# Attention in split float32: two narrow matmuls of the last key tile joined in a bank of their own, and half of the probabilities' low part made on GpSimd

## The chip, the core and the metric

The kernel runs on one core of one Trainium2 chip. Its time is the device time of one execution in microseconds (us). The engines are named as in the profile: PE is TensorE (matmuls), PEld its weight loads, DVE is VectorE, ACT is ScalarE, POOL is GpSimd, SP is SyncE, which here only starts DMAs. Each engine works through its own instructions in the order in which the program gives them; where one waits, those behind it on that engine wait too.

## The reference, cut to what matters

Four batches of 512 rows, 512 wide. The input is layer-normalised, and the normalised rows go through an attention of 16 heads and through a gated feed-forward network; the result is the input plus the product of both.

```python
x  = L0_attn_x                                   # (4, 512, 512)
xn = layernorm(x)
q = einsum('bpd,hde->bphe', xn, W_Q) + b_Q       # k and v alike; 16 heads of 128
scores = where(causal, einsum('bqhe,bkhe->bhqk', q, k) / sqrt(128), -100000.0)
attn = softmax(scores)
z = einsum('bkhe,bhqk->bqhe', v, attn)
s = einsum('bqhe,hed->bqd', z, W_O) + b_O
g = silu((silu((xn @ gate_w.T) * gate_s) * ((xn @ up_w.T) * up_s)) @ down_w.T * down_s)
out = x + s * g
```

## The kernel before, in words

**Split numbers.** Every operand of a matmul is kept as two float32r numbers, a high part (the value cast to float32r) and a low part (the value minus the high part, `Split` in line 28). A product of two such operands is three matmuls: high by high, low by high and high by low (`mm3`, line 90). The high part is usually written by ScalarE and the low part by VectorE, which needs the high part for its subtraction; weights have their low part from GpSimd (`split_w`, line 133).

**The order of the work.** The attention runs inside a manual schedule: the order in the program text is the order on each engine, and the tile framework adds the semaphores. The outer loop (line 525) goes over 64 heads, in the order group of two heads, batch, head of the group. In the iteration of head n stand, one after another:

- `softmax` (line 272): the scores of head n in four query tiles, packed in three PSUM tiles, only the causal part; VectorE adds the mask and takes the row minimum (L298); ScalarE takes the exponential (L312); VectorE the reciprocal of the row sum (L315); GpSimd multiplies by it (L316).
- `look` (a VectorE operation on feed-forward weights, from head 9 on) and the first half of `fill`: projections of v for an even head (`project_v`, L237 and L238 are its evacuations), or output projections of the group before for an odd one (`project_out`, L413).
- `turn_p` (line 319): VectorE transposes the probabilities in 32 by 32 blocks (L330), and a DMA to memory and four back by SyncE's queue finish the transposition. The result is used one head later.
- `split_p` (line 346) for head n-1: the probabilities that have come back, 128 by 4 by 320, are cast in two halves by ScalarE (L357) and their low parts made in two halves by VectorE (L358). In heads 1 to 3 and in the last one it stands before the fill (in head 1 before the softmax), from head 4 on behind `turn_p`.
- `split_pending`: weights that are due are split (ScalarE L134, GpSimd L135); then loads of later weights are started on ScalarE's queue (`prepare_qk`, `prepare_v`, `prepare_o`), which take the staging buffers that the splits before have freed.
- `project` for q and then k of head n+1 (L252 and L255 evacuate).
- `attend` (line 376) for head n-1: the product of v and the probabilities, the step that is changed.
- the second half of `fill`. In heads 0, 2 and 4 the normalised input of the next batch is also transposed (`ln_transpose`, `ln_low`, L222 to L225), and layer-norm statistics and normalisation (L187, L188, L194, L214) stand in heads 0 to 4.

The last head's probabilities are transposed on TensorE instead (`transpose_p`, line 366).

**The attention product before.** Probabilities lie transposed, key rows on the partitions, in ten blocks of 128 by 128: for key tile j the query tiles j to 3. So key tile 0 has a moving operand 512 wide, tile 1 384, tile 2 256 and tile 3, the last, 128. `attend` issues twelve matmuls into one PSUM bank z: for high by high, low by high and high by low the key tiles 0, 3, 1 and 2. Then ScalarE writes the high part of the 512 wide result with the bias (L391) and VectorE its low part (L392).

**Buffers.** PSUM has three banks of the pool `ps_st` (scores and half of the transposed inputs) and five of `ps_mm`, taken in turn by the projections, the output projections, z and the other transposed inputs. The probabilities' high and low parts are two tiles with one buffer each.

**The feed-forward part** follows, for all four batches, with its own order; its weights come by DMAs that GpSimd starts. It is not touched.

Of the kernel before, what the change touches and what calls it, by code (L numbers as in the profile page):

```python
# [10 lines left out]
F32 = mybir.dt.float32  # L11
F32R = mybir.dt.float32r
I32 = mybir.dt.int32
AF = mybir.ActivationFunctionType
ALU = mybir.AluOpType
# [3 lines left out]
P = 128  # L19
HG = 2  # L20
# [22 lines left out]
def kernel(  # L43
# [21 lines left out]
    nc = tc.nc  # L65
    B, S, D = x.shape
    H, E = w_o.shape[0], w_o.shape[1]
    NF = gate_w.shape[0]
    ND = D // P
    NT = S // P  # L70
# [25 lines left out]
    with ExitStack() as at:  # L96
        lnp = at.enter_context(tc.tile_pool(name="lnp", bufs=NT))
        small = at.enter_context(tc.tile_pool(name="small", bufs=8))
# [5 lines left out]
        pp = at.enter_context(tc.tile_pool(name="pp", bufs=1))  # L104
# [3 lines left out]
        ps_mm = at.enter_context(tc.tile_pool(name="ps_mm", bufs=5, space=PSUM))  # L108
# [31 lines left out]
        def weight(pool, shape, name, tag):  # L140
            return Split(
                pool.tile(shape, F32R, name=name + "h", tag=tag + "h"),
                pool.tile(shape, F32R, name=name + "l", tag=tag + "l"),
            )
# [123 lines left out]
        NS = NT * (NT + 1) // 2  # L268
        row = [t * (t + 1) // 2 * P for t in range(NT)]
        slot = [j * NT - j * (j - 1) // 2 for j in range(NT)]  # L270
# [48 lines left out]
        def turn_p(of):  # L319
# [23 lines left out]
                )  # L343
            return raw

        def split_p(raw):
            pt = weight(pp, [P, NS, P], "pt", "pt")
            half = NQ // 2
            for k in range(0, NQ, half):
                src = raw[:, k : k + half].rearrange("p b (s i) -> p b s i", i=Q)  # L350

                def dst(part):
                    return part[:, :, k * Q : (k + half) * Q].rearrange(
                        "p s (b i) -> p b s i", i=Q
                    )

                nc.scalar.copy(dst(pt.hi), src)  # L357
                nc.vector.tensor_tensor(dst(pt.lo), src, dst(pt.hi32), ALU.subtract)  # L358
            return pt

        def transpose_p(of):

            pt = weight(pp, [P, NS, P], "pt", "pt")
            pairs = [(j, t) for j in range(NT) for t in range(j, NT)]
            for s0 in range(0, NS, NT):
                n = min(NT, NS - s0)
                tr = ps_st.tile([P, n, P], F32, name="trp", tag="st")
                for k in range(n):
                    j, t = pairs[s0 + k]
                    nc.tensor.transpose(tr[:, k, :], of[t][:, ts(j, P)], ident)  # L370
                to = pt[:, s0 : s0 + n, :]
                nc.scalar.copy(to.hi, tr)
                nc.vector.tensor_tensor(to.lo, tr, to.hi32, ALU.subtract)
            return pt

        def attend(h, pt, vs):
            z = ps_mm.tile([P, NT, P], F32, name="z", tag="mm")


            todo = []  # L380
            for part, other in (("hi", "hi"), ("lo", "hi"), ("hi", "lo")):
                for j in (0, NT - 1, 1, 2):
                    v = getattr(vs[j], part)[:, ts(h % HG, E)]
                    p_ = getattr(pt, other)[:, slot[j] : slot[j] + NT - j, :]
                    todo.append((z[:, j:, :], v, p_))
            for k, (o, v, p_) in enumerate(todo):
                nc.tensor.matmul(o, v, p_, start=k == 0, stop=k == len(todo) - 1)  # L387
            zT = weight(zp, [P, NT, P], f"z{h}", "z")

            bias = bv_sb[:, h : h + 1]  # L390
            nc.scalar.activation(zT.hi, z, AF.Identity, bias=bias)  # L391
            nc.vector.scalar_tensor_tensor(zT.lo, z, bias, zT.hi32, ALU.add, ALU.subtract)  # L392
            return zT

        acc_in = {}
# [65 lines left out]
        with tc.manual_schedule():  # L461
# [59 lines left out]
            def attend_last(before, pt):  # L521
                g, b, i = before
                zs.setdefault((g, b), []).append(attend(g * HG + i, pt, v_of[g, b]))

            for n, (g, b, i) in enumerate(heads):
                h = g * HG + i
# [20 lines left out]
                if n == 1:  # L547
                    pt = split_p(raw)
                of = softmax(qT, kT)
                if n > 1 and early:  # L550
                    pt = split_p(raw)
# [5 lines left out]
                if not early:  # L557
                    pt = split_p(raw)
# [54 lines left out]
                if nxt is None:  # L613
                    pt = transpose_p(of)
# [6 lines left out]
                if n == len(heads) - 3:  # L621
                    inexact = any_of(low)
            last = (NG - 1, B - 1)
            zs[last].append(attend(H - 1, pt, v_of[last]))
            for t in range(NT):
                project_out(*last, t, zs[last])
# [177 lines left out]
```

## Time and profile before

| | us |
|---|---|
| median of 3 runs | 1223.65 (1223.3 to 1223.92) |
| the profiled execution | 1222.41 |
| its span | 1220.6 |
| PE busy | 1206.5 (99%) |
| DVE busy | 827.1 (68%) |
| ACT busy | 525.3 (43%) |
| POOL busy | 301.7 (25%) |
| granted TensorE clock, mean | 0.998 |

Groups of the profile that the change touches:

| line, engine | what | count | mean ns |
|---|---|---|---|
| L387 PE | attention product, 128 wide, high parts | 64 | 220 |
| L387 PE | the same, 256 / 384 / 512 wide | 64 each | 281 / 391 / 389 |
| L391 ACT | high part of z, 128x512 | 64 | 685 to 689 |
| L392 DVE | low part of z, 128x512 | 64 | 748 to 751 |
| L357 ACT | high part of the probabilities, 128x640 | 126 | 724 |
| L358 DVE | low part of the probabilities, 128x640 | 126 | 1099 (min 772, median 811, max 1916) |
| L135 POOL | low part of a weight, 128x512 | single rows | 1292 to 1879 |
| L316 POOL | normalisation, 128x512 / 128x128 | 64 each | 694 / 409 |

How to read it: a span is the time from the first to the last instruction of the profiled execution, and the execution's own time is a little longer. A matmul's duration includes its way through the array, in which the next one already runs; what it costs is the distance between starts. The mean of L358 hides two kinds of instance, as its median and maximum show. In a row of the timeline the columns are start in us from the span's start, duration in us, engine, line, operation, output and inputs, shape, and in brackets how long the engine had stood idle and what ended that.

### The profile page before, as it was taken

The numbers are of one execution on the slowest core, as the hardware profiler recorded it, in microseconds if no ns is written. First come the engines' busy times: TensorE is split into PE (matmuls) and PEld (weight loads), VectorE is DVE, ScalarE is ACT, GpSimd is POOL, SyncE is SP. The second block draws the span as 40 slices with busy tenths as digits, with TensorE's granted clock in tenths as the row PEclk, the third lists the DMA queues.
The fourth block names the chain that finished last, engine by engine and source line by source line (L and its number), as shares of the span: only waits on it lengthen the run. The fifth ranks groups of instructions, "written<-read, shape, count | busy, mean of one in ns | idle before, by whom it ended". The sixth has DMA issues, their size and how long they took to land.

```text
span 1220.6 us, 18887 instructions
## 1 busy us (share of the span) xinstructions
PE 1206.5 (99%) x6514; PEld 1052.7 (86%) x6514; DVE 827.1 (68%) x2044; ACT 525.3 (43%) x1169; POOL 301.7 (25%) x433
## 2 busy tenths in 40 slices
PE   8999999999999999999999999999999999999997
PEld 8888888888888888888888888888888888888886
DVE  6897777777777777777877676767677533434343
ACT  5654444444445445444544454445444342323231
POOL 4212321232123213321412141214121341212010
PEclk9999999999999999999999999999999999999999
DMA  4454456656665667566655565555544893627241
GB/s 161 138 175 147 145 165 206 206 179 190 190 207 174 203 198 218 181 208 192 211 182 173 178 189 175 177 185 173 173 156 156 272 317 93 207 87 213 80 147 38
DMA packets 117912, 215.55 MB, mean 177 GB/s; under 512 B 13232, under 2 KB 45744, under 8 KB 117808
## 3 DMA queue, kind: packets, MB, share of 16 engines
q1 hardware_dynamic: 74016, 134.51, 34.4%
q10 hardware_dynamic: 29376, 53.26, 14.2%
q0 software_dynamic: 14416, 26.48, 7.9%
q8 instruction: 53, 0.87, 0.3%
q14 instruction: 51, 0.42, 0.1%
HBM read 135.17 MB, written 79.04 MB: 175 GB/s over the span
## 4 chain that ended last, share of the span: by engine, by line
PE 95%; DVE 3%; ACT 1%; DMA 0%; issue 0%; SPq 0%; DVEq 0%; ACTq 0%
PE z L387 10%; PE pd L667 7%; PE pg L667 7%; PE pu L667 7%; PE pso L91 5%; PE psv L91 5%; PE pso L92 5%; PE pso L93 5%; PE psv L93 5%; PE psv L92 5%; PE psq L91 5%; PE psq L92 5%; PE psq L93 5%; PE psk L91 5%; PE psk L92 5%; PE psk L93 5%
## 5 line engine op out<-in xcount | busy, mean ns | idle before, releaser
L316 POOL TENSOR_SCALAR p<-p,rtot 128x512 f32<-128x512 f32 (+3 forms) x256 | 148.2, 598 | 675.1 <-DVE rtot L315 675.1
L312 ACT ACTIVATE p<-p,nmax 128x512 f32<-128x512 f32 (+3 forms) x256 | 140.9, 552 | 147.3 <-DVE nmax L298 147.3
L358 DVE TENSOR_TENSOR ptl<-ptr,pth 128x640 fp32r<-128x640 f32 x126 | 133.7, 1099 | 1.4 <-ACT pth L357 1.4
L330 DVE STREAM_TRANSPOSE sq<-p 128x256 f32<-128x256 f32 x378 | 113.3, 361 | 0.0
L298 DVE CUSTOM_DVE_ANT_0 p<-sc,mask 128x512 f32<-128x512 f32 (+2 forms) x192 | 96.5, 552 | 0.3 <-PE sc L93 0.3
L252 ACT ACTIVATE k<-psk,consts 128x512 fp32r<-128x512 f32 (+1 forms) x65 | 44.2, 681 | 108.7 <-PE psk L93 108.6
L252 ACT ACTIVATE q<-psq,consts 128x512 fp32r<-128x512 f32 (+1 forms) x65 | 44.3, 682 | 97.2 <-PE psq L93 72.6
L357 ACT CAST pth<-ptr 128x640 fp32r<-128x640 f32 x126 | 84.9, 724 | 0.1
L413 DVE TENSOR_TENSOR a<-pso,a 128x512 f32<-128x512 f32 x108 | 72.1, 686 | 17.7 <-PE pso L93 16.4
L255 DVE SCALAR_TENSOR_TENSOR k<-psk,consts,k 128x512 fp32r<-128x512 f32 (+1 forms) x65 | 48.0, 739 | 52.8 <-ACT k L252 52.7
L693 DVE SCALAR_TENSOR_TENSOR hd<-pu,consts,sg 128x512 f32<-128x512 f32 x44 | 33.0, 751 | 66.8 <-PE pu L667 62.2
L315 DVE RECIPROCAL rtot<-tot 128x1 f32<-128x1 f32 x256 | 41.6, 162 | 42.7 <-ACT p L312 36.3
L91 PE MATMUL sc<-k,q 128*128 128x512 f32 (+2 forms) x192 | 65.7, 342 | 1.7 <-DVE xl L225 1.7
L93 PE MATMUL sc<-k,q 128*128 128x512 f32 (+2 forms) x192 | 64.7, 337 | 0.0
L92 PE MATMUL sc<-k,q 128*128 128x512 f32 (+2 forms) x192 | 64.7, 337 | 0.0
L255 DVE SCALAR_TENSOR_TENSOR q<-psq,consts,q 128x512 fp32r<-128x512 f32 (+1 forms) x65 | 47.6, 732 | 7.6 <-ACT q L252 7.6
L312 ACT ACTIVATION_READ_ACCUMULATOR p<-p,nmax 128x1 f32 x256 | 47.8, 187 | 0.0
L91 PEld LDWEIGHTS sc<-k,q 128*128 128x128 f32 x192 | 36.2, 188 | 7.9 <-DVE xl L225 3.5
L723 ACT ACTIVATE o<-o 128x512 f32<-128x512 f32 (+1 forms) x17 | 10.3, 607 | 68.8 <-DVE o L722 68.8
L92 PEld LDWEIGHTS sc<-k,q 128*128 128x128 f32 x192 | 36.2, 189 | 3.6
L93 PEld LDWEIGHTS sc<-k,q 128*128 128x128 f32 x192 | 36.1, 188 | 2.6
L691 ACT ACTIVATE sg<-pg,consts 128x512 f32<-128x512 f32 x44 | 30.3, 688 | 17.0 <-PE pg L667 17.0
(734 smaller groups left out, 3811.6 us busy)
## 6 DMA issues: line engine op xcount, KB each, us to landing
turn<-sq SPq DMA_DIRECT2D x63, 640.0 KB, 3.8
ptr<-turn SPq DMA_DIRECT2D x252, 160.0 KB, 3.4
acc<-a SPq DMA_DIRECT2D x124, 256.0 KB, 3.7
a<-acc ACTq DMA_DIRECT2D x108, 256.0 KB, 2.8
xt<-in_x SPq DMA_DIRECT2D x16, 256.0 KB, 4.1
wor<-in_w_o ACTq DMA_DIRECT2D x16, 256.0 KB, 4.5
fa<-acc SPq DMA_DIRECT2D x16, 256.0 KB, 5.9
fx<-in_x SPq DMA_DIRECT2D x16, 256.0 KB, 6.9
```

What stands on the lines that cost most here:

```text
L91: nc.tensor.matmul(ps, a.hi, b.lo, start=first, stop=False)
L92: nc.tensor.matmul(ps, a.hi, b.hi, start=False, stop=False)
L93: nc.tensor.matmul(ps, a.lo, b.hi, start=False, stop=last)
L252: nc.scalar.activation(q.hi[:, at_], ps[:, at_], AF.Identity, bias=bias[:, h : h + 1])
L255: nc.vector.scalar_tensor_tensor(q.lo[:, at_], ps[:, at_], bias[:, h : h + 1], q.hi32[:, at_], ALU.add, ALU.subtract,)
L298: nc.vector.tensor_tensor_reduce(out=of[t], in0=where[t], in1=add, scale=-SCALE, scalar=BIG, op0=ALU.add, op1=ALU.min, accum_out=nmax[t],)
L312: nc.scalar.activation(of[t], of[t], AF.Exp, bias=nmax[t], scale=-1.0, accum_out=tot)
L316: nc.gpsimd.tensor_scalar(of[t], of[t], rtot, 1.0, ALU.mult, ALU.mult)
L330: nc.vector.transpose(dst.rearrange("p a s i -> p s a i"), src.rearrange("p (s a i) -> p s a i", s=n, i=Q),)
L358: nc.vector.tensor_tensor(dst(pt.lo), src, dst(pt.hi32), ALU.subtract)
L387: nc.tensor.matmul(o, v, p_, start=k == 0, stop=k == len(todo) - 1)
L667: nc.tensor.matmul(ps, l, r, start=first and k == 0, stop=last and k == len(pairs) - 1)
```

## The change

Three things change, all in the attention.

- `attend`: key tiles 0 to 2 go into z as before, in nine matmuls. The last key tile goes into a second bank, z2, 128 by 2 by 128. One matmul, 256 wide, multiplies the high part of v's last tile with the high and the low part of the probabilities' block, which lie side by side in the result; one, 128 wide, adds the low part of v times the high part of the probabilities to the first of the two. So eleven matmuls stand in place of twelve.
- The result leaves in two pieces: query tiles 0 to 2 from z as before, 384 wide; for the last query tile ScalarE copies z2 to memory on the chip (`rest`), VectorE adds its two halves and then the last part of z, and from that sum ScalarE writes the high and VectorE the low part, 128 wide.
- The probabilities' two parts are one tile with a high and a low half (`p_split`), since the joined matmul reads both; and of the two subtractions that make the low part (`split_p`) the first is GpSimd's and the second VectorE's.

```diff
+        def p_split():
+            both = pp.tile([P, 2, NS, P], F32R, name="pt", tag="pt")
+            pt = Split(both[:, 0], both[:, 1])
+            pt.both = both
+            return pt
+
         def split_p(raw):
-            pt = weight(pp, [P, NS, P], "pt", "pt")
+            pt = p_split()
...
                 nc.scalar.copy(dst(pt.hi), src)
-                nc.vector.tensor_tensor(dst(pt.lo), src, dst(pt.hi32), ALU.subtract)
+                on = nc.gpsimd if k == 0 else nc.vector
+                on.tensor_tensor(dst(pt.lo), src, dst(pt.hi32), ALU.subtract)
             return pt

         def transpose_p(of):
-            pt = weight(pp, [P, NS, P], "pt", "pt")
+            pt = p_split()
...
         def attend(h, pt, vs):
             z = ps_mm.tile([P, NT, P], F32, name="z", tag="mm")
+            z2 = ps_mm.tile([P, 2, P], F32, name="z2", tag="mm")
+            last = NT - 1
+            e = ts(h % HG, E)
             todo = []
             for part, other in (("hi", "hi"), ("lo", "hi"), ("hi", "lo")):
-                for j in (0, NT - 1, 1, 2):
-                    v = getattr(vs[j], part)[:, ts(h % HG, E)]
+                for j in range(last):
+                    v = getattr(vs[j], part)[:, e]
                     p_ = getattr(pt, other)[:, slot[j] : slot[j] + NT - j, :]
                     todo.append((z[:, j:, :], v, p_))
             for k, (o, v, p_) in enumerate(todo):
                 nc.tensor.matmul(o, v, p_, start=k == 0, stop=k == len(todo) - 1)
+            s_ = slot[last]
+            nc.tensor.matmul(z2, vs[last].hi[:, e], pt.both[:, :, s_, :], start=True, stop=False)
+            nc.tensor.matmul(z2[:, 0], vs[last].lo[:, e], pt.hi[:, s_, :], start=False, stop=True)
             zT = weight(zp, [P, NT, P], f"z{h}", "z")
             bias = bv_sb[:, h : h + 1]
-            nc.scalar.activation(zT.hi, z, AF.Identity, bias=bias)
-            nc.vector.scalar_tensor_tensor(zT.lo, z, bias, zT.hi32, ALU.add, ALU.subtract)
+
+            def leave(at_, src):
+                nc.scalar.activation(zT.hi[:, at_], src, AF.Identity, bias=bias)
+                nc.vector.scalar_tensor_tensor(
+                    zT.lo[:, at_], src, bias, zT.hi32[:, at_], ALU.add, ALU.subtract
+                )
+
+            leave(slice(0, last), z[:, :last])
+            rest = small.tile([P, 2, P], F32, name="rest", bufs=1)
+            nc.scalar.copy(rest, z2)
+            nc.vector.tensor_tensor(rest[:, 0], rest[:, 0], rest[:, 1], ALU.add)
+            nc.vector.tensor_tensor(rest[:, 1], z[:, last], rest[:, 0], ALU.add)
+            leave(last, rest[:, 1])
             return zT
```

## The prediction

> **What bounds the kernel now.** I read the page first (busy shares and the chain that ended last), then TensorE's waits over the whole run, then the timeline of one ordinary head, and last the timeline where the page's slices show VectorE fullest, the first 100 us.
>
> From the page, shares and chain:
>
> ```profile
> PE 1206.5 (99%) x6514; PEld 1052.7 (86%) x6514; DVE 827.1 (68%) x2044; ACT 525.3 (43%) x1169; POOL 301.7 (25%) x433
> PE 95%; DVE 3%; ACT 1%; DMA 0%; issue 0%; SPq 0%; DVEq 0%; ACTq 0%
> ```
>
> TensorE's own waits in the attention after its start:
>
> ```profile
> PE sc L91 <- DVE xl L225: 1.7, 4, 0.6
> PE tr L222 <- DVE k L255: 0.7, 1, 0.7
> ```
>
> So TensorE is the bound, and it waits only near the start, for VectorE. Between 200 and 960 us it never waits, and a head lasts 14.8 us, of which VectorE is busy 11.15, ScalarE 6.6 and GpSimd 3.3. What a matmul costs is therefore the distance from one start to the next. One attention product, start and duration, and below it where a narrow matmul ends a score tile:
>
> ```profile
> 505.45 0.39 PE L387 MATMUL z<-pth,v_0h 128*128 128x512 f32 x1
> 505.68 0.22 PE L387 MATMUL z<-pth,v_3h 128*128 128x128 f32 x1
> 505.73 0.39 PE L387 MATMUL z<-pth,v_1h 128*128 128x384 f32 x1
> 505.96 0.28 PE L387 MATMUL z<-pth,v_2h 128*128 128x256 f32 x1
> 506.08 0.40 PE L387 MATMUL z<-pth,v_0l 128*128 128x512 f32 x1
> ...
> 511.11 0.34 PE L92 MATMUL sc<-k,q 128*128 128x384 f32 x1
> 511.28 0.33 PE L93 MATMUL sc<-k,q 128*128 128x384 f32 x1
> 511.46 0.28 PE L91 MATMUL sc<-k,q 128*128 128x256 f32 x1
> 511.57 0.28 PE L92 MATMUL sc<-k,q 128*128 128x256 f32 x1
> ```
>
> The reader is to see two things. A 384 wide matmul takes 0.175 between score matmuls, but 0.23 right behind a narrow one, so a narrow matmul costs its own 0.05 to 0.06 and 0.055 in its successor, 0.11 in all. And a 256 wide one costs 0.118, hardly more.
>
> **The change, part by part.**
>
> *TensorE.* Per head, three narrow matmuls (3 x 0.11) become one 256 wide (0.118) and one narrow (0.11): 0.33 - 0.228 = 0.10 to 0.11. I take 0.107. Bounds: 0 if narrow ones cost only their own 0.057 (3 x 0.057 against 0.118 + 0.057), 0.118 if a whole 256 wide slot goes. Over 64 heads: -6.8 us. A rule speaks against this. The Trainium skill (TensorE: Matmul & The Clock Gate, Back-to-back issue gap) gives a warm gap of N/2.4 + 2.5 ns for a matmul alone, about 56 ns at 128 columns and 109 at 256; by that the estimate of the saving is 2 ns a head, 0.1 us in all, and the time would rise. The rows with 0.23 decide against it here.
>
> *Leaving the accumulator.* Before, per head: one ScalarE 128x512 (0.69) and one VectorE 128x512 (0.75). After: ScalarE 384 wide (0.58, between its 0.46 at 256 and 0.69 at 512), copy of the 256 wide bank (0.37, as the v casts) and 128 wide (0.35 to 0.39); VectorE 384 wide 0.62, two 128 wide adds (0.29 each, as the mask add), 128 wide 0.35. VectorE: +0.8 busy, and about 0.4 in which it waits for ScalarE's last piece; ScalarE waits in turn for both adds, with the v casts, the x casts and the exponentials queued behind it. In an ordinary head nobody is late: the z result is used a head or more later, VectorE has 3.6 idle, and the v casts can slip half a microsecond. The new bank moves each of the five in the rotation on by one; in an ordinary head its taker always finds one free.
>
> *Half of the low part on GpSimd.* VectorE loses one of two 0.76 us subtractions in 63 heads. GpSimd's price is in no row: 128x512 costs it 1.29 alone and 1.88 at worst beside VectorE, so per element 1.6 and 2.35 for 640; the written side goes in runs of 32, for which GpSimd has no row, while VectorE's same subtraction shows no penalty. I take 1.6, and leave the top open to 3.2, twice the flat price. Normally it lies beside VectorE's transposes:
>
> ```profile
> 56.00 2.55 POOL L135 TENSOR_TENSOR wo0l<-wor,wo0h 128x512 fp32r<-128x512 f32 x2 [1.51 <-ACT wo0h L134]
> ...
> 532.00 3.12 POOL L135 TENSOR_TENSOR wo4l<-wor,wo4h 128x512 fp32r<-128x512 f32 x2 [1.50 <-ACT wo4h L134]
> ```
>
> ```profile
> 56.49 1.79 DVE L330 STREAM_TRANSPOSE sq<-p 128x256 f32<-128x256 f32 x6
> ...
> 502.65 1.52 DVE L358 TENSOR_TENSOR ptl<-ptr,pth 128x640 fp32r<-128x640 f32 x2
> ...
> 532.25 3.56 DVE L358 TENSOR_TENSOR ptl<-ptr,pth 128x640 fp32r<-128x640 f32 x2
> ```
>
> The transposes are not slowed beside a GpSimd subtraction (1.79, as everywhere), the low part is: 1.78 each in place of 0.76. So where both halves run at once, VectorE gains nothing: 1.78 for one half against 1.52 for two. That is so in heads 1 to 3 and in the last, where split_p stands before the transposes.
>
> *The first heads, where VectorE is the bound.* These rows carry the sum:
>
> ```profile
> 45.65 0.75 DVE L392 SCALAR_TENSOR_TENSOR z0l<-z,consts,z0h 128x512 fp32r<-128x512 f32 x1 [0.78 <-ACT z0h L391]
> 46.32 0.69 DVE L187 BATCH_NORM_STATS2 st<-xt 128x6 f32<-128x512 f32 x1
> ...
> 61.45 0.75 DVE L255 SCALAR_TENSOR_TENSOR k<-psk,consts,k 128x512 fp32r<-128x512 f32 x1
> 62.11 0.74 DVE L392 SCALAR_TENSOR_TENSOR z1l<-z,consts,z1h 128x512 fp32r<-128x512 f32 x1
> ...
> 63.43 2.47 DVE L225 TENSOR_TENSOR xl<-tr,xh 128x512 fp32r<-128x512 f32 x4
> ```
>
> (1) z of head 0 holds VectorE 1.2 longer and starts 0.35 sooner (nine matmuls, not twelve): the layer-norm statistics behind it, the root, the table load, the exponentials and the casts of the probabilities (done at 54.87) come 0.85 later. (2) The product of head 1, which began at 55.18, now begins about 55.7, and its low group waits for VectorE's half, 1.78 beside GpSimd, done at 57.5: 0.75 more. (3) VectorE has no idle time from 54.3 to 67.8, so all of it slips by 57.5 - 55.9 = 1.6: the k low part ends at 63.8. Then z of head 1: 0.53 + 0.25 + 0.3 until both adds are done, ScalarE's last piece 0.4, the two v casts and the first x cast that stood behind it, 1.1: the first xl starts near 66.4 in place of 63.43. The score tiles wait for xl, so TensorE is 3.0 late there. (4) In head 3 the fourth output projection now takes the bank that q leaves, freed by VectorE at 77.9 + 3.0 + 0.25, where TensorE comes at 80.4: 0.75. (5) The same wait as in (3) in head 4, where VectorE has 1.8 idle: 0.2. Sum 3.95, say +3.9; ends +1.5 (if (3) hides half and (4) all) and +5.
>
> *The end.* Nothing follows that would cover the last low part: the normalisation on GpSimd ends at 960.9, its half at 962.5, and the product wants it at 961.4: 1.1. The transposed split behind it on ScalarE and VectorE starts later by as much, and the last z starts 0.24 sooner: +1.0, ends +0.3 and +2.
>
> *Seven heads before a new group.* ScalarE's queue stands there behind two weight loads that wait for GpSimd:
>
> ```profile
> 119.02 0.33 ACTq L130 DMA_DIRECT2D wqr<-in_w_q  x1
> 120.85 0.33 ACTq L130 DMA_DIRECT2D wkr<-in_w_k  x1
> 121.23 0.69 ACT L252 ACTIVATE q<-psq,consts 128x512 fp32r<-128x512 f32 x1 [3.10 <-PE psk L93]
> ```
>
> With a half of h us from 116.5 on, then 1.88 and 1.29 for the weights, the load goes at 119.7 + h, q's low part ends at 121.5 + h, and TensorE wants q's bank for the fourth v at 123.7: it waits if h is over 2.2, then 7 x (h - 2.2). At 1.6: nothing.
>
> **Sum**: -6.8 + 3.9 + 1.0 = -1.9. The profiled execution took 1222.41 with a span of 1220.6; the median of the three runs is 1223.65, 1.2 above it. Span 1218.7, execution 1220.5, median about 1221.7.
>
> **The rivals.** (A) The start costs half: VectorE and ScalarE interleave better than I lined them up, +1.5. For it: much of (3) is waits put end to end. Time 1219.3. (B) GpSimd's half takes about 2.5 us: 7 x 0.3 and 0.9 at each end of the attention, near 1224.5. (C) Slower: GpSimd's half takes 3.2 us, because of its written runs of 32: 7 x 1.0 in the seven heads, 1.6 more at the end and 0.9 in head 1, about 1231. It decides from h = 2.9 (7 x 0.7, over the 1.9 gained, is past the bound). Against it: no engine's row shows a price for these runs. (D) The change does not do what it says: the narrow matmuls' 0.055 returns behind the joined one, and only the costs remain, 1228. Against it: the 256 wide score matmuls stand 0.118 apart with nothing lost.
>
> **How the numbers follow.** Least that a measurement of this kernel tells from no change: 0.2%, 2.45 us. Base case 0.52 (it lies close to that bound: 0.22 faster, 0.30 same), A 0.18 (faster), B 0.14 (same), C 0.12 (slower), D 0.04 (slower). Faster 0.40, same 0.44, slower 0.16. The range goes from A with the higher saving, 1218.3, up past B to 1226.5; outside it about 2 in 10. The base case alone: 1219.9 to 1223.3.
>
> **What the changed kernel's profile would show.** Attention products 1.80 long in place of 1.91, and heads 14.69 apart in place of 14.8 between 200 and 900 us. GpSimd's half near 1.6 us, beside the transposes. TensorE's waits for VectorE, ScalarE and GpSimd up from 2.4 to about 6 us, nearly all before 100 us. The fifth score product (95.48 before) 3.5 later. Wrong if: products stay at 1.9 (D), TensorE waits appear in the seven heads (B, C), or the start is not later by more than 2 (A).

## The result: 0.25% slower, and not where the forecast had looked

| | us |
|---|---|
| median before | 1223.11 (13 runs, 1222.14 to 1224.08) |
| median after | 1225.73 (13 runs, 1224.55 to 1229.63) |
| ratio | 1.0025, 95% interval 1.0017 to 1.0033 |
| profiled execution before / after | 1222.41 / 1225.68 |
| its span before / after | 1220.6 / 1223.9 |
| forecast | 1221.7 (1218.3 to 1226.5) |

The time lies inside the range, the sign was wrong: 2.6 us lost where 1.9 gained were forecast.

### The profile after

The line of the page with the busy shares, and the shares of the chain that ended last:

```profile
PE 1201.8 (98%) x6450; PEld 1046.0 (85%) x6450; DVE 794.2 (65%) x2173; ACT 554.1 (45%) x1297; POOL 392.6 (32%) x496
PE 20%; DVE 0%; ACT 0%; issue 0%
```

TensorE has 4.7 us less work, VectorE 33 less, GpSimd 91 more; TensorE is still the bound. But the chain, 95% TensorE before, now breaks off after 20%: followed back from the end it gets no further than the feed-forward part. That is the first sign that something in front of that part is new. TensorE's own waits, from the list of waits after:

```profile
PE sc L91 <- DVE xl L225: 3.0, 4, 1.9
...
PE pg L691 <- SPq L824: 1.8, 1, 1.8
...
PE z L397 <- DVE pt L365: 1.1, 2, 0.6
PE z L397 <- ACT pt L363: 0.7, 1, 0.7
```

The columns are the sum, how many, and the longest. Three of these lie where the forecast had them, at the start and in the last heads. The line of pg, 1.8 us at the first matmul of the feed-forward part, was 0.9 before.

The attention product in the middle of the run, from the timeline:

```profile
506.91 0.39 PE L397 MATMUL z<-pt,v_0h 128*128 128x512 f32 x1
...
508.50 0.28 PE L399 MATMUL z<-pt,v_3h 128*128 128x256 f32 x1
508.61 0.22 PE L400 MATMUL z<-pt,v_3l 128*128 128x128 f32 x1
508.68 0.33 PE L91 MATMUL psv<-wv4l,xh 128*128 128x256 f32 x1
```

From the first start to where the v projection behind it may go it lasts 1.8 us, not 1.9. Between 200 and 800 us TensorE is busy without a gap, and heads come 0.11 us closer than before.

Where the two profiled executions part, from the starts in both timelines (difference to the kernel before, in us):

| up to | before | after | difference | added on this stretch |
|---|---|---|---|---|
| 7th score product (first matmul) | 110.60 | 115.02 | +4.42 | +4.42, the start |
| 64th score product | 954.47 | 952.43 | -2.04 | -6.46, 57 heads at 0.113 |
| last matmul of the attention (pso) | 972.68 | 971.47 | -1.21 | +0.83, the attention's tail |
| first matmul of the feed-forward part (pg) | 974.00 | 973.67 | -0.33 | +0.88, the wait for its weight |
| end of VectorE's last operation | 1215.73 | 1217.05 | +1.32 | +1.65, half clock after that wait |
| end of the span | 1220.58 | 1223.91 | +3.33 | +2.01, the end of the program |

Up to the attention's end the change does gain, 1.21 us. All of that and 3.3 more goes in three places behind it, which the change does not touch in the text.

**The feed-forward weights.** GpSimd starts their loads. Before (GpSimd's first load, then TensorE's first matmul):

```profile
961.20 0.58 POOL L651 DMA_DIRECT2D wg0h<-in_gate_w  x1 [0.30 <-POOL p L316]
974.00 0.47 PE L667 MATMUL pg<-xl,wg0h 128*128 128x512 f32 x1 [0.94 <-PE pso L93]
```

and after:

```profile
969.18 0.58 POOL L675 DMA_DIRECT2D wg0h<-in_gate_w  x1 [10.00 <-DVE z15l L407]
973.67 0.47 PE L691 MATMUL pg<-xl,wg0h 128*128 128x512 f32 x1 [1.81 <-SPq L824]
```

GpSimd now stands for 10 us until VectorE has made the very last piece of the attention, which reads `rest`. The reason lies in the places of the tiles in the built program. `rest` is in the attention's pool `small`, at bytes 110112 to 111136 of each partition; when the attention's pools are given back, the feed-forward weights are laid over them, and wu3h takes bytes 109600 to 111648. The framework puts the wait for `rest` at the head of the branch, in front of all weight loads, not in front of wu3h alone. Before the change nothing at these addresses was read that late.

**Half clock.** The same start in stretches of 2 us (busy us of PE, PEld, DVE, ACT, POOL with their counts, then the granted TensorE clock, the DMA engines' share, GB/s):

```profile
973.00:975.00 2.00, 1.33 (x6) 1.14 (x7) 0.00 (x0) 0.00 (x0) 1.34 (x3) 0.98 1.11 321
975.00:977.00 2.00, 2.00 (x6) 1.52 (x5) 0.00 (x0) 0.57 (x1) 0.51 (x2) 0.50 1.15 365
977.00:979.00 2.00, 2.00 (x7) 1.58 (x6) 0.00 (x0) 1.40 (x2) 0.75 (x2) 0.67 1.15 381
```

From 974.9 to 978.3, 3.4 us, TensorE has half its clock, after the wait is over; before, the clock is 1.00 there. Matmuls that come every 0.23 us come every 0.43: 1.65 us are lost.

What decides is how the wait lies in time, as the fourteen traces of this case show together. Within each trace the granted clock changes only at times that are whole multiples of 3.413 us apart (in the change 66.97, 70.38, 974.91 and 978.33). Cut into stretches by that grid, from 20 us to the last matmul, TensorE has no matmul for 1.76 to 2.14 us in each of the six stretches that a fall follows (1.81 in the one that ends at 974.91), and for at most 1.62 us in any other. The profile is one execution; in another the grid may divide the same wait, and then by this count the clock would not fall.

**The end of the program.** SyncE closes with a row of semaphore waits after the last output has landed. From the trace, start in us, of the kernel after:

```
1220.53 1220.60 1220.67 1220.74 1220.80 1220.89 1220.97   | 1222.68 1222.77 1222.83 ...
```

Before, the twelve stand 0.06 apart from 1218.93 to 1219.62, without the 1.71 us hole. In the hole one packet of 8 KB passes on the queue that the profile calls "q14 instruction"; such packets pass in closing rows without a hole as well (before the change at 1218.94, in short_code below at 1219.03), so the packet alone proves nothing.

### The profile page after: what moved, and what is told of

The parts are those of the page before. It is cut to its first block, busy times and chain, and to the rows that moved or that the text cites. A ratio compares the mean times of both kernels' runs of the same rounds, so it can differ in the third digit from the quotient of the medians.

```text
span 1223.9 us, 19306 instructions
## 1 busy us (share of the span) xinstructions
PE 1201.8 (98%) x6450; PEld 1046.0 (85%) x6450; DVE 794.2 (65%) x2173; ACT 554.1 (45%) x1297; POOL 392.6 (32%) x496
## 5 line engine op out<-in xcount | busy, mean ns | idle before, releaser
L316 POOL TENSOR_SCALAR p<-p,rtot 128x512 f32<-128x512 f32 (+3 forms) x256 | 145.7, 587 | 588.4 <-DVE rtot L315 588.4
L365 POOL TENSOR_TENSOR pt<-ptr,pt 128x640 fp32r<-128x640 f32 x63 | 99.4, 1577 | 20.9 <-ACT pt L363 20.6
L363 ACT CAST pt<-ptr 128x640 fp32r<-128x640 f32 x126 | 85.0, 724 | 0.1
L437 DVE TENSOR_TENSOR a<-pso,a 128x512 f32<-128x512 f32 x108 | 69.4, 681 | 0.1
L91 PE MATMUL sc<-k,q 128*128 128x512 f32 (+2 forms) x192 | 66.4, 346 | 3.0 <-DVE xl L225 3.0
L365 DVE TENSOR_TENSOR pt<-ptr,pt 128x640 fp32r<-128x640 f32 x63 | 61.9, 983 | 3.4 <-ACT pt L363 3.4
L397 PE MATMUL z<-pt,v_0h 128*128 128x512 f32 x128 | 50.9, 397 | 2.1 <-DVE pt L365 1.1
L91 PEld LDWEIGHTS sc<-k,q 128*128 128x128 f32 x192 | 36.4, 189 | 9.7 <-DVE xl L225 5.4
L397 PE MATMUL z<-pt,v_1h 128*128 128x384 f32 x128 | 43.0, 336 | 0.0
```

The costliest lines, as they stand in the source:

```text
L91: nc.tensor.matmul(ps, a.hi, b.lo, start=first, stop=False)
L316: nc.gpsimd.tensor_scalar(of[t], of[t], rtot, 1.0, ALU.mult, ALU.mult)
L365: on.tensor_tensor(dst(pt.lo), src, dst(pt.hi32), ALU.subtract)
L437: nc.vector.tensor_tensor(a, ps, a, ALU.add)
```

## The experiments

The theory after this reading: the change loses 4.4 at the start and 0.8 in the tail as forecast, and three things that the forecast did not have: weights that wait for `rest`, the clock that falls after this wait, and code that SyncE has to fetch in its closing row. Rivals: GpSimd's half costs all along; the late start of the feed-forward part has another reason; the hole belongs to the semaphores named in it. Ratios are to the kernel before, measured beside them on the same chip; its medians there were 1222.5 (rest_kept, join_only, half_only, old_start), 1222.7 (join_late, old_two, short_code, kept_busy) and 1222.3 (the others).

### rest_kept: another place for `rest`

```diff
-            rest = small.tile([P, 2, P], F32, name="rest", bufs=1)
+            rest = const.tile([P, 2, P], F32, name="rest", tag="rest")
```

> The change whole, but the small tile of the new evacuation (rest) lies in the pool that is never given back, so that no FFN weight is laid over it. Theory: the FFN's first weight load is then issued right after GpSimd's last half (about 959.5 us, was 969.18), TensorE's wait ahead of the FFN falls from 1.81 to the 0.94 of before, and the 3.4 us at half clock after it go, which cost 1.7: 2.5 less than the change, about 1223.2 (1222.5 to 1224). Rival: the FFN starts late for another reason (the branch, the load itself), then the load may come earlier but the time stays at 1225.7.

Measured: 1223.54, ratio 1.0009 (1.0000 to 1.0018). The two rows that moved:

```profile
959.73 0.58 POOL L675 DMA_DIRECT2D wg0h<-in_gate_w  x1
973.43 0.47 PE L691 MATMUL pg<-xl,wg0h 128*128 128x512 f32 x1 [0.94 <-PE pso L93]
```

The first load follows GpSimd's half at once, TensorE waits 0.94 as before the change, the clock stays at 1.00 there, and from the first feed-forward matmul to VectorE's last end it takes 241.73 us, as before (241.73; 243.38 in the change). The wait and the half clock behind it came from the tile's place; 2.0 us of the loss are these by the ratios (2.5 in the two profiles).

### join_only and half_only: one part alone

join_only:

```diff
-                on = nc.gpsimd if k == 0 else nc.vector
+                on = nc.gpsimd if False else nc.vector
```

half_only, twelve matmuls in z and one evacuation as before:

```diff
+            join = False
...
-                for j in range(last):
+                for j in range(last) if join else (0, last, 1, 2):
...
+            if not join:
+                leave(slice(0, NT), z)
+                return zT
```

> The joined matmul and its evacuation alone; the low part of the probabilities all on VectorE, as before the change; rest lies where the change has it. Theory: attention products 1.81, the start costs about 2.5 in place of 4.4, the attention's tail about 0.1 in place of 0.8, the FFN's start is late as in the change: about 1223.1 (1222 to 1224.5). Rival (GpSimd's half is what costs, all along): 1217, the whole saving.

> GpSimd's half of the low part alone; twelve matmuls in one bank and one evacuation, as before the change. Theory: products 1.91 as before, no wait in the steady heads, about 1 more at the start and 0.9 in the attention's tail, the FFN starts at once: about 1225 (1224 to 1226). Rival (GpSimd's half costs all along): 1232.

Measured: join_only 1222.77, ratio 0.9999 (0.9990 to 1.0008); half_only 1227.07, ratio 1.0035 (1.0021 to 1.0049). Score products' lateness against the kernel before, counted from each run's own first score product (us):

| score product | change | rest_kept | join_only | half_only | old_two | put_off | old_start |
|---|---|---|---|---|---|---|---|
| 4th | +1.63 | +1.71 | +0.87 | +0.84 | +0.05 | +1.67 | +0.03 |
| 5th | +3.86 | +3.95 | +4.48 | +1.70 | +0.90 | +3.19 | +0.08 |
| 7th | +4.39 | +4.49 | +4.26 | +1.83 | +1.43 | +3.09 | +0.05 |
| 64th | -2.07 | -1.97 | -2.17 | +1.82 | -5.03 | -3.24 | -6.30 |

half_only stays at +1.82 from the 7th head to the last: GpSimd's half costs nothing in the steady heads and gains nothing either, so the rival falls. Its effect is 1.8 at the start, 0.44 in the tail (last matmul of the attention 2.27 later), and 1.76 in SyncE's closing row (below), which I had not expected of it and which makes up most of the 2 us by which it missed its forecast; of the 4.6 us between the medians some 0.5 is left and was not followed. join_only has the full saving, and at the start it loses as much as both parts together: the parts do not add, since either makes VectorE and ScalarE late in the same stretch. Some of its loss at the start may be the clock's: its profile has half clock there from 66.1 to 73.0 us, twice as long as the change's. Its 4.26 instead of the expected 2.5 is balanced by the closing row, which has no hole there (below).

### old_start and old_two: the first heads as before

old_start, on rest_kept (old_two has 2 in place of 6):

```diff
-                on = nc.gpsimd if k == 0 else nc.vector
+                on = nc.gpsimd if k == 0 and n_ >= 6 else nc.vector
+            join = k_ >= 6
```

Here n_ counts the calls of `split_p` and k_ those of `attend`; where join is false, the product and its evacuation are those of before.

> rest kept as in rest_kept, and the first six heads (products and low parts) done as before the change. Theory: the 4.4 us that the change loses by its seventh score product are not lost, six heads give up 0.11 each: 3.8 less than rest_kept, about 1219.4 (1218.5 to 1220.5). Rival: what the start loses is given back by something later anyway: as rest_kept.

> As rest_kept, but the products and low parts of the first two heads alone are done as before the change. Theory (the prediction's steps (1) to (3): the evacuations of heads 0 and 1 and the low part of head 1 make the start late): the fifth score product begins at most 1 us later than before the change, not 3.9, and the time is about 3 below rest_kept, 1220.5. Rival: VectorE has no idle time until the fifth head, so the heads behind lose it in their turn: at most 1 below rest_kept, 1222.5.

Measured: old_start 1219.38, ratio 0.9973 (0.9963 to 0.9983), 4.2 below rest_kept; old_two 1221.77, ratio 0.9991 (0.9982 to 1.0000). In old_start nothing is lost at the start and the 0.113 per head stays. In old_two the fifth score product is 0.90 late, as expected, and its profile is 3.06 ahead of rest_kept at the last head; its median is only 1.8 lower (2.0 counted from the kernel before on each chip) and lies between the forecast, 1220.5, and the rival's 1222.5. So two heads, the first and the second, carry 3 of the 4.4 us by the profile, about 2 by the medians, as steps (1) to (3) of the prediction had it, and the rest comes in the heads behind.

### put_off: the piece that blocks ScalarE

How the start goes in the change, from the timelines of VectorE and ScalarE:

```profile
64.61 0.29 DVE L415 TENSOR_TENSOR rest<-z,rest 128x128 f32<-128x128 f32 x1
65.00 0.40 ACT L406 ACTIVATE z1h<-rest,consts 128x128 fp32r<-128x128 f32 x1 [5.65 <-DVE rest L415]
...
65.82 2.06 ACT L224 CAST xh<-tr 128x512 fp32r<-128x512 f32 x4
...
66.45 1.89 DVE L225 TENSOR_TENSOR xl<-tr,xh 128x512 fp32r<-128x512 f32 x3
```

ScalarE stands idle for 5.65 us in front of a piece of 0.40, because VectorE's adds come late, and the casts of the normalised x, which were ready to go, stand behind it. put_off is rest_kept with this piece placed behind those casts in the three heads with layer-norm transposes:

```diff
-            leave(last, rest[:, 1])
+            owed.append(lambda: leave(last, rest[:, 1]))
+            if not put_off:
+                settle()
...
                         ln_low(b + 1, t)
+                    settle()
```

> As rest_kept, but in the three heads ahead of a layer-norm's transposes ScalarE's last piece of the evacuation and VectorE's low part of it come after the casts of the normalised x, not before. Theory (step (3) of the prediction: ScalarE stands 5.65 us at that piece, with two v casts and the x casts behind it): the first xl of head 3 comes 0.8 earlier, 65.7 in place of 66.45, and the time is about 1 below rest_kept, 1222.5 where the kernel before is 1222.6. Rival (VectorE alone sets the start): as rest_kept, 1223.6.

Measured: 1221.98, ratio 0.9999 (0.9990 to 1.0008), against 1.0009 for rest_kept: 1.2 us less. In its timeline ScalarE's last x cast, the piece behind it and VectorE's first xl now stand so:

```profile
64.44 0.59 ACT L224 CAST xh<-tr 128x512 fp32r<-128x512 f32 x1 [0.73 <-PE tr L222]
64.92 0.40 ACT L406 ACTIVATE z1h<-rest,consts 128x128 fp32r<-128x128 f32 x1
...
65.32 2.47 DVE L225 TENSOR_TENSOR xl<-tr,xh 128x512 fp32r<-128x512 f32 x4
```

The first xl starts at 65.32, not 66.45 (0.9 earlier, counted from the first score product), and the seventh score product is 1.4 less late than in rest_kept. What is left, 3.1, was not taken apart; VectorE works without a break there from 55.58 on, and in front of that it waits 1.08 for ScalarE's cast of the probabilities.

### short_code and long_code: the hole in SyncE's closing row

In every run the hole sits at the same place of SyncE's program, counted over all its instructions, those of the untaken branch too:

| kernel | SyncE's instructions | semaphores before the hole | hole, us |
|---|---|---|---|
| before, join_only, join_late, late_weights | 1087 or 1095 | none | 0 |
| change, rest_kept, put_off, kept_busy, long_code | 1115 | 7 | 1.71 to 1.78 |
| old_two | 1114 | 8 | 1.80 |
| half_only | 1113 | 9 | 1.76 |
| old_start | 1111 | 11 | 1.46 |
| short_code, best | 1093, 1089 | none | 0 |

One instruction less, and the hole comes one semaphore later. The change makes SyncE's program 28 instructions longer, all of them waits on semaphores (442 in place of 414), most of them in front of the loads that bring the turned probabilities back. The two experiments change the branch for inexact weights, which is never taken here, and nothing that is executed:

short_code, on rest_kept:

```diff
-                nc.sync.dma_start(out=raw, in_=src)
+                load = nc.scalar if name.startswith("wd") else nc.sync
+                load.dma_start(out=raw, in_=src)
```

long_code, on the kernel before, for the weights wd4 to wd10:

```diff
+                    for k in range(4):
+                        c = slice(k * D // 4, (k + 1) * D // 4)
+                        nc.sync.dma_start(out=raw[:, c], in_=src[:, c])
```

> As rest_kept, but in the branch that is not taken (weights that are not exact) the eleven down weights load on ScalarE's queue, not on SyncE's: 22 instructions less in SyncE's program, none of them ever executed. Theory: the 1.6 us that SyncE stands still inside its closing row of semaphores are a wait for code at a fixed place of its program; with 22 instructions less that place lies behind the end, the gap is gone and the closing row runs through as before the change: 1.6 below rest_kept, about 1221.9. Rival: the gap is a wait for one of the named semaphores: as rest_kept, 1223.5.

> The kernel before the change, in which only the branch that is not taken is longer: 28 instructions more in SyncE's program (seven weights load in four pieces each), none ever executed, so that SyncE's program has as many instructions as in the change, 1115. Theory: SyncE's closing row of semaphores stands still for 1.5 to 1.7 us after its seventh semaphore, as in the change: 1.6 over the kernel before, about 1224.2. Rival (the gap belongs to what the change executes): 1222.6.

Measured: short_code 1221.89, ratio 0.9994 (0.9985 to 1.0003), 1.65 below rest_kept (1.8 counted from the kernel before on each chip), closing row without a hole. long_code 1224.01, ratio 1.0013 (1.0004 to 1.0022), 1.7 above the kernel before, with a hole of 1.73 after the seventh semaphore. Code that never runs moves the time by 1.7 us both ways. That the place in the program decides is shown. That SyncE waits there for code is an inference from this; the packet in the hole does not decide it, since short_code has such a packet in its closing row and no hole.

### kept_busy and late_weights: the wait and the clock apart

kept_busy, on the change:

```diff
+                    if exact and (b, f, n) == (0, 0, "g"):
+                        for _ in range(8):
+                            nc.tensor.matmul(
+                                ps[n], xnT[0].hi[:, 0, :P], xnT[0].hi[:, 0, :], start=True, stop=True
+                            )
```

late_weights, on the kernel before:

```diff
+            if len(attend_n) == B * H:
+                rest = small.tile([P, 2, P], F32, name="rest", bufs=1)
+                nc.scalar.copy(rest[:, 0], zT.hi32[:, 0])
+                nc.vector.tensor_copy(rest[:, 1], rest[:, 0])
```

> The change whole, and ahead of the FFN's first matmul eight 512 wide matmuls on data that is there, into the bank that the first real one begins anew: 1.8 us of TensorE work that is thrown away, in the time in which TensorE waits for the first FFN weight. Theory: the wait stays, but the 3.4 us at half clock after it are gone: 1.65 below the change, about 1224.1. Rival (the clock falls for another reason, or the FFN's first matmuls are slow because the weights still come in): as the change, 1225.7, or above.

> The kernel before the change, in which only the last head also writes a 1 KB tile into the small pool and reads it (one ScalarE and one VectorE copy of 128x128), so that the FFN's weights, laid over that memory, have to wait for it as in the change. Theory: the first FFN weight is issued near 969.5 in place of 961.2, the first FFN matmul comes up to 0.9 later, and 3.4 us at half clock follow where the wait is as long as in the change (1.65): 1.0 to 2.6 over the kernel before, about 1225 where that is 1222.6. Rival (the late weights cost nothing by themselves): 1222.6.

Measured: kept_busy 1226.31, ratio 1.0027 (1.0017 to 1.0038); late_weights 1222.41, ratio 1.0001 (0.9992 to 1.0010). Both expectations on the time missed.

In kept_busy the clock does stay at 1.00 at that place and the feed-forward part takes 241.63 us, not 243.38. But the eight matmuls could not start in the wait: their bank is one that VectorE has still to empty, so they began 1.27 us after the last output projection's start, and the first real matmul came 3.16 after it in place of 2.20. By the profile that should still leave a gain of 0.8, which the medians don't show; the profiled execution was the slowest of its eight and had lost 1.2 more between 175 and 510 us, 0.6 of it in waits of v projections for VectorE's q. That profile also has half clock at the start, from 67.4 to 74.2 us, and its seventh score product is 0.6 later than the change's. A gain of 0.8 is below what the interval tells apart. For the time this run is inconclusive.

In late_weights the first load came at 968.56, as late as meant, but TensorE's wait was only 1.20, and the clock did not fall. There the load stands 3.5 us ahead of the last matmul of the attention, in the change 2.3, since its evacuation ends later. So the late weight alone cost 0.26 there, and the fall came only with a longer wait. Over all runs, at this place: no fall after waits of 0.94 and 1.20, a fall after 1.81 (change) and 2.1 (join_only), each of which lies whole in one stretch of the clock's grid.

### join_late and best: what can be had

join_late, on rest_kept:

```diff
-                on = nc.gpsimd if k == 0 else nc.vector
+                on = nc.gpsimd if False else nc.vector
...
+            join = k_ >= 6
```

best, on rest_kept, with the edit of short_code as well:

```diff
-                on = nc.gpsimd if k == 0 else nc.vector
+                on = nc.gpsimd if k == 0 and 6 <= n_ < 62 else nc.vector
...
+            join = k_ >= 6
```

> The joined matmul alone, from the seventh head on, rest kept out of the FFN's memory, the low part all on VectorE as before the change. Theory: 58 heads give 0.11 each, the start, the FFN's start and SyncE's closing sequence stand as before the change, the attention's tail loses 0.3 at most: 6.2 less than the kernel before, about 1216.3 where that is 1222.5. Rival (without GpSimd's half VectorE is too full for the longer evacuation): no better than old_start, 1219.4 or more.

> All that the runs point to at once: joined matmul from the seventh head on, GpSimd's half from the seventh head on but not in the last, rest kept out of the FFN's memory, SyncE's untaken branch 22 instructions shorter. Theory: old_start less 0.8 in the attention's tail and less 1.6 in SyncE's closing row: about 1217.0. Rival (the gap at the end or the tail come back elsewhere): 1218.5 or more.

Measured: join_late 1217.02, ratio 0.9950 (0.9937 to 0.9964); best 1218.25, ratio 0.9965 (0.9952 to 0.9979). Both beat both kernels; the two intervals overlap. best missed its 1217.0 and came close to its rival's 1218.5. The tail costs nothing in either (last matmul of the attention 18.2 behind the 64th score product, as before; 19.0 in the change). In both profiles some of the saving is lost in single heads, in TensorE's waits between 200 and 510 us, of join_late (whose profiled execution is the slowest of its five):

```profile
PE z L402 <- DVE pt L365: 0.8, 2, 0.4
```

and of best:

```profile
PE psv L91 <- DVE q L255: 0.7, 1, 0.7
```

The first are heads in which VectorE alone has to make the low part; the second is one of the seven heads that the prediction had named, with GpSimd's half ahead of the weights. Each way has a margin that is used up now and then. Joining the matmuls is worth having; GpSimd's half is not needed for it.

## Why the prediction was wrong, by its own steps

- **TensorE's saving** (0.107 a head, 6.8): right. 0.113 a head from the 7th to the 64th. The Trainium skill (TensorE: Matmul & The Clock Gate, Back-to-back issue gap) speaks of a matmul alone, and the estimate from its gap was 2 ns; the rows decide against it here, as the prediction took it. Rival D falls.
- **GpSimd's half** (1.6 us): right, 1.58 on average; rivals B and C, which needed 2.5 and 3.2, fall. **The seven heads** (nothing): right in the change's profile, but thin; two other runs waited 0.6 and 0.7 in such heads.
- **The first heads** (+3.9): the mechanism was right down to the row, the size too small. The first xl came at 66.45 for a forecast of 66.4. But the sum counts the first six heads' saving apart, so the 4.42 measured stand for 5.1 of its +3.9: the score product at 95.48 before, which the prediction calls the fifth and which is the sixth as the table above counts, was 3.9 late, not 3.5, and the seventh lost 0.5 more, which no item had. Rival A falls.
- **The end** (+1.0): 0.83.
- **The sum's last line**, "Span 1218.7", is the step that failed. It carries what the attention gains through to the span, as if nothing behind the attention could change, because no line of the feed-forward part was edited. Up to there the forecast was 0.7 us off (-1.9, measured -1.21), and that it was so close is partly luck: the start cost 1.2 more, the matmuls saved 0.3 more and the end cost 0.2 less. Behind it came +0.88, +1.65 and +2.01, of which it has no term and no rival: a new tile in a pool whose memory is used again, the clock after the wait, the length of SyncE's program. The prediction followed the instructions that are written out, and not the waits that the framework adds to them: 28 on SyncE, and GpSimd's at the head of the branch. short_code, which is the change without the longer wait, its clock and the hole, comes to 0.9994 (0.9985 to 1.0003) of the kernel before, some 0.7 us less: the sign of the forecast, with about a third of its size and not clear of no change.
- **The range**: that 1225.73 lies in it is luck. Its upper part was there for rival B, which did not happen, and not for what did. B's own terms (7 x 0.3 and twice 0.9, on 1221.7) also add up to 1225.6, not to the 1224.5 given.
- **TensorE's waits "from 2.4 to about 6 us, nearly all before 100 us"**: 5.0 there, and 0.8 in the tail; the 0.9 more at the feed-forward start it did not expect. One row was read loosely, with nothing resting on it: GpSimd is busy 3.8 us a head between 200 and 956 us, not 3.3.

Of the 2.01 at the end 1.7 are the hole. The remaining 0.3, an output that landed 0.7 later after its issue and a shorter step behind it, were not followed further.

## What to carry to other kernels

A new tile also has an address: where a pool is given back and its memory used again, look at who is laid over the new tile and when it is last read, and keep small late scratch out of such pools. A gain of a few us in 1200 is of the size of what the framework adds unseen, so count the waits of every engine's program before and after, those of queues that only start DMAs too. And where the first heads have no slack, leave them as they are: the saving of 58 heads is worth more than that of 64 with 4 us lost ahead.

## What the runs showed of the hardware that I had not expected

- TensorE's clock fell to half for 3.4 us after a wait of 1.81 us that was already over, and the length of a wait alone does not decide. The change waits 1.93 us in front of 67.19 and the clock falls; rest_kept waits the same 1.93 in front of 67.77, but a step of the grid falls into that wait, at 66.80, the stretches on its two sides hold 1.62 and 1.36 us of idle time, and the clock stays. Idle time inside one stretch of 3.413 us tells the two apart in all traces: a fall from 1.76 up, none up to 1.62. The Trainium skill (TensorE: Matmul & The Clock Gate, The HAM clock gate) has a free-running window of 3413 ns, which agrees with the grid. Its rule of thumb (HAM oscillation) speaks of idle gaps over some 3.4 us; here about half of that was enough, and the measurement decides.
- The same fall at the start cost little. The change's profile has half clock from 67.0 to 70.4 us, rest_kept has 1.00 there, and their seventh score products are equally late (+4.39 and +4.49). But short_code, which runs the same program up to there as rest_kept, is at +4.66 with one such stretch, and kept_busy, the same as the change up to there, at +4.96 with two; so 0 to 0.6 us may be the clock's. At the feed-forward start, where TensorE is the bound, one stretch cost 1.65.
- The length of a program that is not executed can cost: a hole of 1.5 to 1.8 us in SyncE's closing row at one fixed place of its program, which moves by one semaphore with each instruction.
